# Second layer in place and by chunks, last attention block by token groups, maxima over partitions on TensorE, and one normalization moved to GpSimd

## Chip, cores and metric

One core of a Trainium2 chip runs the whole program. The metric is device time in microseconds (us). Before the change three runs took 737.27, 738.0 and 739.08 us, median 738.0. Five engines work side by side, each through its own queue in program order: TensorE (PE) multiplies matrices, VectorE (DVE) and ScalarE (ACT) do elementwise work and reductions, GpSimd (POOL) does elementwise work, and SyncE (SP) only issues transfers. ACT can issue transfers too. An engine passes its work on to another through semaphores, and an instruction that waits at the head of a queue holds all that stand behind it.

## What is computed

A gated block: cross-attention of 4096 tokens of width 512 over a context of 77 rows, then a feed-forward net of width 2048 whose two linear layers round their input and their weights to integers, with one scale for a whole tensor. Cut to what matters:

```python
def _quant_per_tensor(x):
    scale = jnp.maximum(jnp.max(jnp.abs(x)), 1e-6) / 127.0
    return round(x / scale), scale

def _qlinear(x2d, w, b):
    xq, sx = _quant_per_tensor(x2d)
    wq, sw = _quant_per_tensor(w)
    return (xq @ wq.T + b) * (sw * sx)

x = x + tanh(g_xattn) * attention(layernorm(x), ctx, ctx)   # 16 heads of 32
n = layernorm(x)
h = gelu(_qlinear(n, w1, b1))
x = x + tanh(g_ffn) * _qlinear(h, w2, b2)
```

Each maximum runs over a whole tensor. So the first layer can't begin before the last token has left the attention, and the second can't begin before the last hidden value is known.

## The kernel before

The tokens are cut into NB = 8 blocks of 512, each held on chip as four groups of 128 tokens: `X[i]`, [128, 4, 512] f32. Everything happens in one program, in three stages.

**Attention.** A loop over the blocks, inside it eight steps `s`. The order on PE and DVE is partly written out by hand (`tc.issue_after`); a scheduling layer places the rest. In each step `softmax` (L248) gets scores from PE, subtracts the maximum on DVE, takes the exponential on ACT and the sum on DVE, and has GpSimd multiply by the reciprocal (L275); PE transposes the result (`transpose_a`), multiplies by the values (`apply_v`), and projects (`project_o`, L307) into `po`; DVE adds that to X (L317). `norm2` (L321) makes the statistics of the new X (`mean2`, `rstd2`; GpSimd takes the power -1/2 at L140) and the largest normalized value of the block, `xmax`. In blocks 1 to 4 the weights of the feed-forward net are loaded, their maxima are taken (`weight_max`, L350), and they are rounded to `w1q` and `w2q`. `scale_of` (L142) turns maxima of 128 partitions into one scale: DVE reduces within a partition, GpSimd reduces over the partitions with `partition_all_reduce` (L148), and DVE makes the scale and its inverse. For the last block there is no next block to work beside: four projections, then one `norm2` for all four groups (L468 to L470).

**First layer.** `quantize_x` (L496) normalizes a block again into `xs`, rounds it into `xq` (adding and subtracting a large constant), transposes it on PE into `px`, and DVE copies it to `xqT`. For each block, 16 hidden chunks of 128 follow: four matmuls into half of a `ph` tile (two tiles of two halves), the gelu on ACT with scale `s1` (L536), and for each pair of chunks a maximum on DVE (`hmax`, L543). Four chunks make a tile `G` of 1 MB. The tiles of blocks 0 to 5 go out to DRAM (L554, issued by SP); the eight of blocks 6 and 7 are held in the eight buffers of `gpool` (HELD = 8).

**Second layer.** Blocks in the order 6, 7, 0, ... 5 (L566). Each tile, held or loaded back into a free `gpool` buffer as `Gb` (L573, issued by SP), is scaled in place on ACT (L574) and rounded on DVE into `hq` (L575; two buffers). For each token group GpSimd adds the bias to X (L579), 16 matmuls accumulate in `po`, which the profile calls `pf` (two PSUM buffers), DVE makes `o = pf * s2 + X` (L590; two buffers of `opool`), and ACT's queue issues the store of `o` (L592).

Of the kernel before, what the change touches and what calls it, by code (L numbers as in the profile page):

```python
# [8 lines left out]
F32 = mybir.dt.float32  # L9
# [6 lines left out]
P = 128  # L16
# [23 lines left out]
def tile_flamingo_gated_block(  # L40
# [78 lines left out]
    identb = const.tile([P, P], BF16, name="identb")  # L119
    nc.vector.tensor_copy(identb, ident)  # L120
    mhalf = const.tile([P, NT], F32, name="mhalf")
    nc.gpsimd.memset(mhalf, -0.5)
# [4 lines left out]
    rstd2 = const.tile([P, NB, NT], F32, name="rstd2")  # L127
    xmax = const.tile([P, NB], F32, name="xmax")
    hmax = const.tile([P, NB, GT, 2], F32, name="hmax")

    def layernorm_stats(xb, mv, rstd, name):

        n = xb.shape[1]
        st = small.tile([P, n, 6], F32, tag="st", name=f"st_{name}")
        for t in range(n):
            nc.vector.bn_stats(st[:, t, :], xb[:, t, :])
            nc.vector.bn_aggr(mv[:, t, :], st[:, t, :])
        ve = small.tile([P, n], F32, tag="ve", name=f"ve_{name}")
        nc.vector.tensor_scalar(ve, mv[:, :, 1], EPS, None, ALU.add)
        nc.gpsimd.tensor_tensor(rstd, ve, mhalf[:, :n], ALU.pow)  # L140

    def scale_of(maxima, name):  # L142


        m = const.tile([P, 1], F32, name=f"m_{name}")
        nc.vector.tensor_reduce(m, maxima, AX.X, ALU.max)
        g = const.tile([P, 1], F32, name=f"g_{name}")
        nc.gpsimd.partition_all_reduce(g, m, P, bass_isa.ReduceOp.max)  # L148
        s = const.tile([P, 1], F32, name=f"s_{name}")
        nc.vector.tensor_scalar(s, g, MIN_RANGE, 1.0 / QP, ALU.max, ALU.mult)  # L150
        inv = const.tile([P, 1], F32, name=f"inv_{name}")
        nc.vector.reciprocal(inv, s)
        return s, inv

    def quantize(dst, src, inv):

        nc.vector.tensor_scalar(src, src, inv, MAGIC, ALU.mult, ALU.add)
        nc.vector.tensor_scalar(dst, src, MAGIC, None, ALU.subtract)

# [4 lines left out]
    with actx:  # L164
# [155 lines left out]

        def norm2(i):  # L321
            xb = X[i]
            layernorm_stats(xb, mean2[:, i, :, :], rstd2[:, i, :], f"f{i}")
            tm = small.tile([P, NT], F32, tag="tm", name=f"tm{i}")
            for t in range(NT):
                xn = work.tile([P, D], F32, tag="xn", name=f"xf{i}_{t}")
                nc.vector.tensor_scalar(
                    xn,
                    xb[:, t, :],
                    mean2[:, i, t, 0:1],  # L330
                    rstd2[:, i, t : t + 1],
                    ALU.subtract,
                    ALU.mult,
                )
                nc.vector.tensor_reduce(
                    tm[:, t : t + 1], xn, AX.X, ALU.max, apply_absolute_value=True
                )
            nc.vector.tensor_reduce(xmax[:, i : i + 1], tm, AX.X, ALU.max)

# [10 lines left out]
        def weight_max(name, j):  # L350
            if j == 0:
                wmax[name] = const.tile([P, 4], F32, name=f"max_{name}")
            nc.vector.tensor_reduce(
                wmax[name][:, j : j + 1],
                wraw[name, j],
                AX.XY,
                ALU.max,
                apply_absolute_value=True,
            )
            if j == 3:  # L360
                s_w[name], inv_w[name] = scale_of(wmax[name], name)

# [6 lines left out]
        def weight_step(i, s):  # L369
            j, odd = divmod(s, 2)  # L370
            if i == 1 and odd:
                weight_max("w1", j)
            if i == 2 and odd:
                quantize(w1q[:, :, j * TB : (j + 1) * TB], wraw["w1", j], inv_w["w1"])
# [31 lines left out]
        for i in range(NB):  # L406
            for s in range(2 * NG):
                last = None
                if s + 1 < 2 * NG:
                    last = softmax(i, s + 1)  # L410
                elif i + 1 < NB:
                    last = softmax(i + 1, 0)
# [39 lines left out]
                if s == 7 and i > 0:  # L452
                    norm2(i - 1)
                if last is not None:
# [10 lines left out]
            if i == 2:  # L465
                load_w("w2", w2_piece, range(2))
        apply_v(NB - 1, NG - 1)
        for t in range(NT):  # L468
            project_o(NB - 1, t)
        norm2(NB - 1)  # L470
    s_w1, s_w2 = s_w["w1"], s_w["w2"]


    s_x, inv_x = scale_of(xmax, "x")
    s1 = const.tile([P, 1], F32, name="s1")
    nc.vector.tensor_tensor(s1, s_x, s_w1, ALU.mult)
    b1s = const.tile([P, FC], F32, name="b1s")
    nc.vector.tensor_scalar(b1s, b1_sb, s1, None, ALU.mult)

    gpool = ctx.enter_context(tc.tile_pool(name="gpool", bufs=HELD))  # L480
    hidden_dram = ctx.enter_context(
# [7 lines left out]

    held, stored = {}, {}  # L490
    with ExitStack() as fctx:
        fwork = fctx.enter_context(tc.tile_pool(name="fwork", bufs=2))
        ps_h = fctx.enter_context(tc.tile_pool(name="ps_h", bufs=2, space=PSUM))
        ps_x = fctx.enter_context(tc.tile_pool(name="ps_x", bufs=2, space=PSUM))

        def quantize_x(i):  # L496
            xs = fwork.tile([P, NT, D], F32, tag="xs", name=f"xs{i}")
            xq = fwork.tile([P, NT, D], BF16, tag="xq", name=f"xq{i}")
            xqT = fwork.tile([P, KC, TB], BF16, tag="xqT", name=f"xqT{i}")
            for t in range(NT):  # L500
                nc.vector.tensor_scalar(
                    xs[:, t, :],
                    X[i][:, t, :],
                    mean2[:, i, t, 0:1],
                    rstd2[:, i, t : t + 1],
                    ALU.subtract,
                    ALU.mult,
                )
            quantize(xq, xs, inv_x)
            for t in range(NT):  # L510
                px = ps_x.tile([P, KC, P], BF16, tag="px", name=f"px{i}_{t}")
                for kc in range(KC):
                    nc.tensor.transpose(px[:, kc, :], xq[:, t, kc * P : (kc + 1) * P], identb)
                nc.vector.tensor_copy(xqT[:, :, t * P : (t + 1) * P], px)
            return xqT

        xqT = quantize_x(0)
        for i in range(NB):
            cur = xqT
            if i + 1 < NB:  # L520
                xqT = quantize_x(i + 1)
            for a in range(GT):
                G = gtile(f"G{i}_{a}")
                for v in range(GF // 2):
                    ph = ps_h.tile([P, 2, TB], F32, tag="ph", name=f"ph{i}_{a}_{v}")
                    for u in range(2):
# [15 lines left out]
                        )  # L542
                    nc.vector.tensor_reduce(  # L543
                        hmax[:, i, a, v : v + 1],
                        G[:, 2 * v : 2 * v + 2, :],
                        AX.XY,
                        ALU.max,
                        apply_absolute_value=True,
                    )
                if i * GT + a >= NB * GT - HELD:  # L550
                    held[i, a] = G
                else:
                    stored[i, a] = hidden_dram.tile([P, GF, TB], F32, name=f"h{i}_{a}")
                    nc.sync.dma_start(stored[i, a], G)  # L554
    s_h, inv_h = scale_of(hmax.rearrange("p b a v -> p (b a v)"), "h")
    s2 = const.tile([P, 1], F32, name="s2")
# [3 lines left out]


    hpool = ctx.enter_context(tc.tile_pool(name="hpool", bufs=2))
    opool = ctx.enter_context(tc.tile_pool(name="opool", bufs=2))
    ps_o = ctx.enter_context(tc.tile_pool(name="ps_o", bufs=2, space=PSUM))
    first = NB - HELD // GT
    for i in [*range(first, NB), *range(first)]:  # L566
        hq = hpool.tile([P, FC, TB], BF16, tag="hq", name=f"hq{i}")
        for a in range(GT):
            if (i, a) in held:
                G = held[i, a]  # L570
            else:
                G = gtile(f"Gb{i}_{a}")
                nc.sync.dma_start(G, stored[i, a])  # L573
            nc.scalar.activation(G, G, AF.Copy, bias=MAGIC, scale=inv_h)  # L574
            nc.vector.tensor_scalar(  # L575
                hq[:, a * GF : (a + 1) * GF, :], G, MAGIC, None, ALU.subtract
            )
        for t in range(NT):
            nc.gpsimd.tensor_tensor(X[i][:, t, :], X[i][:, t, :], b2_sb, ALU.add)  # L579
            po = ps_o.tile([P, D], F32, tag="po", name=f"pf{i}_{t}")  # L580
            for fc in range(FC):
                nc.tensor.matmul(  # L582
                    po,
                    hq[:, fc, t * P : (t + 1) * P],
                    w2q[:, fc, :],
                    start=(fc == 0),
                    stop=(fc == FC - 1),
                )
            o = opool.tile([P, D], F32, tag="o", name=f"o{i}_{t}")
            nc.vector.scalar_tensor_tensor(o, po, s2, X[i][:, t, :], ALU.mult, ALU.add)  # L590
            r = i * TB + t * P
            nc.scalar.dma_start(out[r : r + P, :], o)  # L592

# [61 lines left out]
```

## Time and profile before

| What | From the profile |
|---|---|
| profiled execution | 735.06 us, of which the span from first to last instruction is 733.3 us |
| mean granted PE clock over the span | 0.977 |
| busy: PE, DVE, ACT, POOL | 670.1, 516.0, 342.4, 198.8 us |
| attention, to the end of the last `po` | to 448.4 us |
| first layer, from the first matmul into `ph` to PE's last | 467.4 to 594.4 us |
| second layer, from the first matmul into `pf` to PE's last | 601.3 to 729.3 us |
| loads `Gb`, 24 of 1 MB | 4.7 / 7.5 / 10.9 us from issue to landing (min / median / max) |
| stores of `out`, 32 of 256 KB | 2.0 / 2.7 / 10.4 us |

A profile page names a group of instructions by its line in the code, engine, operation and tiles (`out<-in`, buffer numbers left out). A timeline row has its start, its length, and in brackets how long the engine sat idle before it and what released it. A row of waits reads: who waited, for whom, us in total, number of times, longest. The clock row gives the share of full speed that PE was granted. PE's ends are modelled, and some matmul records are missing, so counts of matmuls in a row can be a little low.

### The profile page before, as it was taken

To read this page: it belongs to the slowest core of one execution; us is meant where nothing else is said; L and a number is where in the kernel's file an instruction comes from. 1 tells how busy PE (TensorE), PEld (TensorE's weight loads), DVE (VectorE), ACT (ScalarE), POOL (GpSimd) and SP (SyncE) were. 2 spreads that over 40 slices of the span, in tenths; PEclk is the share of its full clock that TensorE was granted. 3 is DMA by queue.
4 is the path that set the end of the run, shared out by engine and by line. 5 is a ranking of instruction groups with operands and counts; after the bars stand their busy time and mean duration, and the time that the engine had idled before them with its cause. 6 is when DMAs were issued, how large, how long until landed. Compare 5 with 4: busy or idle time off the path is not lost.

```text
span 733.3 us, 7847 instructions
## 1 busy us (share of the span) xinstructions
PE 670.1 (91%) x2873; PEld 332.7 (45%) x2896; DVE 516.0 (70%) x807; ACT 342.4 (47%) x467; POOL 198.8 (27%) x161
## 2 busy tenths in 40 slices
PE   4999999999999899999999994699999969889897
PEld 2655545454544454555555541344444424334343
DVE  3563688789798699677677576999986666665442
ACT  1444444334433433444344420377777877655500
POOL 3133332342331442333332320000000009980000
PEclk9999999999999999999999998799999979989999
DMA  9901100111320321100000000166666019888621
GB/s 287 341 0 57 59 1 1 58 58 58 114 87 29 115 78 43 52 0 1 0 1 2 0 1 0 53 258 263 278 260 265 1 50 404 348 296 327 253 86 72
DMA packets 26430, 85.40 MB, mean 116 GB/s; under 512 B 3531, under 2 KB 3531, under 8 KB 20248
## 3 DMA queue, kind: packets, MB, share of 16 engines
q1 hardware_dynamic: 19912, 75.15, 26.7%
q10 hardware_dynamic: 6480, 9.76, 3.7%
q8 instruction: 23, 0.38, 0.2%
q14 instruction: 15, 0.12, 0.0%
HBM read 51.34 MB, written 33.55 MB: 116 GB/s over the span
## 4 chain that ended last, share of the span: by engine, by line
PE 64%; DVE 19%; DMA 6%; POOL 5%; ACT 5%; issue 2%; SPq 0%; POOLq 0%; DVEq 0%; ACTq 0%
PE ph L529 16%; PE pq L238 10%; PE po L310 10%; PE pf L582 10%; PE pta L288 6%; PE ps L254 6%; DMA out_y<-o 5%; POOL e L275 3%; PE pc L297 3%; DVE mx L263 2%; DVE sm L272 2%; DVE e L267 2%; ACT G L574 1%; DVE hq L575 1%; DVE o L590 1%
## 5 line engine op out<-in xcount | busy, mean ns | idle before, releaser
L275 POOL TENSOR_TENSOR e<-e,rs 128x616 f32<-128x616 f32 x64 | 78.9, 1234 | 247.1 <-DVE rs L274 184.5
L582 PE MATMUL pf<-w2q,hq 128*128 128x512 bf16 x502 | 117.7, 393 | 17.2 <-DVE o L590 9.6
L529 PE MATMUL ph<-xqT,w1q 128*128 128x512 bf16 x499 | 121.2, 378 | 2.4 <-ACT G L536 1.6
L238 PE MATMUL pq<-xnT,wq_sb 128*128 128x512 f32 x256 | 119.8, 605 | 0.7 <-ACT xnT L230 0.7
L289 ACT COPY aT<-pta 77x512 f32<-77x512 f32 x128 | 73.1, 581 | 93.8 <-PE pta L288 93.6
L310 PE MATMUL po<-wo_sb,cT 128*128 128x512 f32 x256 | 116.4, 593 | 0.0
L536 ACT ACTIVATE G<-ph,b1s,s 128x512 f32<-128x512 f32 x128 | 99.5, 778 | 25.8 <-PE ph L529 20.6
L288 PEld LDWEIGHTS pta<-ident,e 128*77 128x77 f32 x512 | 59.9, 148 | 67.5 <-POOL e L275 33.0
L288 PE MATMUL pta<-ident,e 128*77 128x128 f32 x512 | 79.3, 281 | 12.1 <-POOL e L275 9.7
L543 DVE TENSOR_REDUCE hmax<-G 128x1 f32<-128x1024 f32 x64 | 75.1, 1214 | 20.1 <-ACT G L536 19.9
L582 PEld LDWEIGHTS <-hq 128*128 128x128 bf16 x512 | 51.1, 100 | 83.8 <-issue 19.1
L263 DVE TENSOR_REDUCE mx<-ps 128x8 f32<-128x616 f32 x64 | 50.4, 787 | 44.0 <-PE ps L254 44.0
L529 PEld LDWEIGHTS <-w1q 128*128 128x128 bf16 x512 | 49.0, 97 | 67.9 <-issue 17.6
L254 PE MATMUL ps<-kb,qT 128*128 128x308 f32 x256 | 78.8, 428 | 0.5 <-ACT kb L193 0.4
L270 ACT ACTIVATE e<-e 128x616 f32<-128x616 f32 x64 | 45.9, 716 | 55.8 <-DVE e L267 51.4
L272 DVE TENSOR_REDUCE sm<-e 128x8 f32<-128x616 f32 x64 | 50.5, 790 | 27.9 <-ACT e L270 27.7
L238 PEld LDWEIGHTS pq<-xnT,wq_sb 128*128 128x128 f32 x256 | 46.7, 193 | 50.7 <-issue 47.5
L310 PEld LDWEIGHTS po<-wo_sb,cT 128*128 128x128 f32 x256 | 46.5, 190 | 46.5 <-issue 45.1
L590 DVE SCALAR_TENSOR_TENSOR o<-pf,s,x 128x512 f32<-128x512 f32 x32 | 23.9, 747 | 59.9 <-DMA out_y<-o 37.4
L574 ACT ACTIVATE Gb<-Gb,inv_h 128x2048 f32<-128x2048 f32 x24 | 47.2, 1997 | 31.8 <-DVE o L590 31.6
L267 DVE TENSOR_TENSOR e<-ps,mx 128x616 f32<-128x616 f32 x64 | 50.9, 796 | 6.0 <-POOL e L275 3.4
L579 POOL TENSOR_TENSOR x<-x,b_sb 128x512 f32<-128x512 f32 x32 | 52.6, 1679 | 7.0 <-issue 7.0
(73 smaller groups left out, 612.9 us busy)
## 6 DMA issues: line engine op xcount, KB each, us to landing
h<-G SPq DMA_DIRECT2D x24, 1024.0 KB, 3.9
Gb<-h SPq DMA_DIRECT2D x24, 1024.0 KB, 7.5
raw_w<-in_w2T SPq DMA_DIRECT2D x8, 1024.0 KB, 5.0
out_y<-o ACTq DMA_DIRECT2D x32, 256.0 KB, 2.7
x<-in_x SPq DMA_DIRECT2D x7, 1024.0 KB, 5.0
raw_w<-in_w1T SPq DMA_DIRECT2D x4, 1024.0 KB, 9.7
x<-in_x SPq DMA_DIRECT2D x4, 256.0 KB, 5.8
wq_sb<-in_wqT ACTq DMA_DIRECT2D x1, 1024.0 KB, 11.2
```

Of the source, the lines that this page charges most:

```text
L238: nc.tensor.matmul(pq, wq_sb[:, kc, g * P : (g + 1) * P], xnT[i][:, kc, :], start=(kc == 0), stop=(kc == KC - 1),)
L254: nc.tensor.matmul(ps[:, u, :GK], qT[i, g][:, t * P : (t + 1) * P], kblk[i // NBB][:, g, :], start=True, stop=True,)
L267: last["DVE"] = nc.vector.tensor_tensor(e4, sc, mx[:, :, :, None].to_broadcast([P, 2, HG, NK]), ALU.subtract).ins
L272: nc.vector.tensor_reduce(sm, e4, AX.X, ALU.add)
L275: last["POOL"] = nc.gpsimd.tensor_tensor(e4, e4, rs[:, :, :, None].to_broadcast([P, 2, HG, NK]), ALU.mult).ins
L288: nc.tensor.transpose(pt[:NK, j, :], es[i, s][:, u, j, :], ident)
L289: nc.scalar.copy(aT[i, g][:, :, t * P : (t + 1) * P], pt[:NK, :, :])
L310: nc.tensor.matmul(po, cT[i, g][:, t * P : (t + 1) * P], wo_sb[:, g, :], start=(g == 0), stop=(g == NG - 1),)
L529: nc.tensor.matmul(ph[:, u, :], w1q[:, kc, fc * P : (fc + 1) * P], cur[:, kc, :], start=(kc == 0), stop=(kc == KC - 1),)
L536: nc.scalar.activation(G[:, 2 * v + u, :], ph[:, u, :], AF.Gelu, bias=b1s[:, fc : fc + 1], scale=s1,)
L543: nc.vector.tensor_reduce(hmax[:, i, a, v : v + 1], G[:, 2 * v : 2 * v + 2, :], AX.XY, ALU.max, apply_absolute_value=True,)
L582: nc.tensor.matmul(po, hq[:, fc, t * P : (t + 1) * P], w2q[:, fc, :], start=(fc == 0), stop=(fc == FC - 1),)
```

## The change

- `scale_of` no longer uses GpSimd. DVE multiplies the identity by the column of maxima, PE multiplies a matrix of ones by that diagonal, which puts all 128 maxima into each partition's row of a PSUM tile, and DVE takes the maximum of the row. For the weights the call moves to the first step of the next block.
- The last attention block is handled group by group: statistics after each projection, and the maximum of one group after the statistics of the next. The gelu's table is loaded on ACT by a one-column activation (`warm`) right after the last `cT`.
- Block 0's normalization for the first layer, `xs`, is put on GpSimd, with a raised priority and behind the last product of the softmax. Its rounding goes group by group, the last two groups partly on ACT, which also does the four copies to `xqT`. Other blocks keep DVE; their normalization stands behind the rounding of the block ahead.
- The very last pair's `hmax` is taken in two halves.
- The second layer adds into X and stores from X; `opool` is gone, `ps_o` has four buffers, and SP's queue issues the stores. In its first block the chunk is the outer loop and the four groups the inner one, and the first chunk is rounded by DVE alone.
- Several pools of the later stages get `reuse_waits="tile"`, and `gpool` is put on the other side of the memory.

The diff, cut to its core:

```diff
-    def scale_of(maxima, name):
+    def scale_of(maxima, name, psum, tag):
         m = const.tile([P, 1], F32, name=f"m_{name}")
         nc.vector.tensor_reduce(m, maxima, AX.X, ALU.max)
+        diag = small.tile([P, P], F32, tag="diag", name=f"diag_{name}", bufs=1)
+        nc.vector.tensor_scalar(diag, ident, m, None, ALU.mult)
+        pg = psum.tile([P, 512], F32, tag=tag, name=f"pg_{name}")
+        nc.tensor.matmul(pg[:, :P], ones, diag, start=True, stop=True)
         g = const.tile([P, 1], F32, name=f"g_{name}")
-        nc.gpsimd.partition_all_reduce(g, m, P, bass_isa.ReduceOp.max)
+        nc.vector.tensor_reduce(g, pg[:, :P], AX.X, ALU.max)
...
-            if j == 3:
-                s_w[name], inv_w[name] = scale_of(wmax[name], name)
...
+            if i in (2, 4) and s == 0:
+                name = "w1" if i == 2 else "w2"
+                s_w[name], inv_w[name] = scale_of(wmax[name], name, ps_p, "pp")
...
+        warm = small.tile([P, 1], F32, tag="warm", name="warm")
+        nc.scalar.activation(warm, cT[NB - 1, NG - 1][:, 0:1], AF.Gelu)
         for t in range(NT):
             project_o(NB - 1, t)
-        norm2(NB - 1)
+            last = norm2_stats(NB - 1, t, t + 1)
+            if t > 0:
+                with tc.issue_after(last):
+                    norm2_max(NB - 1, t - 1, t)
+        norm2_max(NB - 1, NT - 1, NT)
...
+        def quantize_x(i, xs, n):
+            xq = fwork.tile([P, NT, D], BF16, tag="xq", name=f"xq{i}")
+            xqT = fwork.tile([P, KC, TB], BF16, tag="xqT", name=f"xqT{i}")
+            for t0 in range(0, NT, n):
+                v, vq = xs[:, t0 : t0 + n, :], xq[:, t0 : t0 + n, :]
+                if n == 1 and t0 >= NT // 2:
+                    nc.scalar.activation(v, v, AF.Copy, bias=MAGIC, scale=inv_x)
+                    last = nc.vector.tensor_scalar(vq, v, MAGIC, None, ALU.subtract).ins
+                else:
+                    last = quantize(vq, v, inv_x)
+                for t in range(t0, t0 + n):
...
+                    if n == 1:
+                        nc.scalar.copy(dst, px)
+                    else:
+                        nc.vector.tensor_copy(dst, px)
+            return xqT, last
+        with tc.issue_after(last_product), tc.high_priority(offset=300):
+            xs = normalize_x(0, nc.gpsimd)
+        s_x, inv_x = scale_of(xmax, "x", ps_g, "pg")
+        xqT, last = quantize_x(0, xs, 1)
...
-    opool = ctx.enter_context(tc.tile_pool(name="opool", bufs=2))
-    ps_o = ctx.enter_context(tc.tile_pool(name="ps_o", bufs=2, space=PSUM))
+    ps_o = ctx.enter_context(tc.tile_pool(name="ps_o", bufs=NT, space=PSUM))
...
+            done = 0
+            if (i, a) == (first, 0):
+                quantize(hq[:, 0, :], G[:, 0, :], inv_h)
+                done = 1
+            rest = G[:, done:, :]
+            nc.scalar.activation(rest, rest, AF.Copy, bias=MAGIC, scale=inv_h)
             nc.vector.tensor_scalar(
-                hq[:, a * GF : (a + 1) * GF, :], G, MAGIC, None, ALU.subtract
+                hq[:, a * GF + done : (a + 1) * GF, :], rest, MAGIC, None, ALU.subtract
             )
...
+        if i == first:
+            for fc in range(FC):
+                for t in range(NT):
+                    accumulate(t, fc)
         for t in range(NT):
-            nc.gpsimd.tensor_tensor(X[i][:, t, :], X[i][:, t, :], b2_sb, ALU.add)
...
-            o = opool.tile([P, D], F32, tag="o", name=f"o{i}_{t}")
-            nc.vector.scalar_tensor_tensor(o, po, s2, X[i][:, t, :], ALU.mult, ALU.add)
+            y = X[i][:, t, :]
+            nc.gpsimd.tensor_tensor(y, y, b2_sb, ALU.add)
+            if i != first:
+                for fc in range(FC):
+                    accumulate(t, fc)
+            nc.vector.scalar_tensor_tensor(y, po[t], s2, y, ALU.mult, ALU.add)
             r = i * TB + t * P
-            nc.scalar.dma_start(out[r : r + P, :], o)
+            nc.sync.dma_start(out[r : r + P, :], y)
```

`normalize_x(i, engine)` (L517 of the changed kernel) is the loop of four normalizations that stood in `quantize_x`, L501 before and L520 after; `accumulate(t, fc)` is one matmul of L582, with `po[t]` allocated at its first chunk.

## The prediction

> **What bounds the kernel now.** I read the page first, then the waits, then the stretches in which TensorE (PE) is not fed. The page has PE at 91% of the span, so only what leaves PE idle, or running slowly, can be won. From the waits:
>
> ```profile
> DVE o L590 <- DMA out_y<-o: 37.4, 10, 7.4
> ACT Gb L574 <- DVE o L590: 31.6, 14, 6.1
> PE pf L582 <- DVE o L590: 9.6, 6, 2.9
> PE pf L582 <- DVE hq L575: 6.8, 1, 6.8
> ```
>
> The chain to see: a store of `out` (256 KB beside the 1 MB loads) holds one of two `o` buffers; VectorE (DVE) waits for it, and ScalarE (ACT), which issues the stores in order, and PE, which has two PSUM buffers, wait for DVE. PE's own timeline of the second layer, with the idle time before each piece in brackets:
>
> ```profile
> 601.25 24.27 PE L582 MATMUL pf<-w2q,hq 128*128 128x512 bf16 x94 [6.83 <-DVE hq L575]
> 626.16 3.61 PE L582 MATMUL pf<-w2q,hq 128*128 128x512 bf16 x16 [0.64 <-DVE o L590]
> 630.59 7.07 PE L582 MATMUL pf<-w2q,hq 128*128 128x512 bf16 x31 [0.82 <-DVE o L590]
> 639.34 3.61 PE L582 MATMUL pf<-w2q,hq 128*128 128x512 bf16 x16 [1.69 <-DVE o L590]
> 645.84 23.82 PE L582 MATMUL pf<-w2q,hq 128*128 128x512 bf16 x94 [2.88 <-DVE o L590]
> 670.34 14.22 PE L582 MATMUL pf<-w2q,hq 128*128 128x512 bf16 x63 [0.68 <-DVE o L590]
> 687.45 41.86 PE L582 MATMUL pf<-w2q,hq 128*128 128x512 bf16 x188 [2.89 <-DVE o L590]
> ```
>
> At the end, where nothing disturbs, DVE's L590 rows follow each other by 3.45 us (722.50, 725.95, 729.40), which is one group of 16 matmuls. 32 groups make 110.4 us; the stage took 729.3 - 601.25 = 128.05. The six waits are 9.6 of the missing 17.65. The table by stretches (columns: length; PE, weight load, DVE, ACT, GpSimd busy; granted clock; DMA share; GB/s) shows most of the rest:
>
> ```profile
> 597.00:601.00 4.00, 0.00 (x0) 0.00 (x0) 2.06 (x6) 3.07 (x2) 0.35 (x1) 0.53 0.00 0
> 605.00:608.00 3.00, 3.00 (x10) 1.19 (x9) 2.01 (x2) 3.00 (x3) 3.00 (x2) 0.59 0.97 352
> 612.00:616.00 4.00, 3.95 (x19) 1.82 (x19) 1.85 (x2) 3.23 (x2) 4.00 (x3) 1.00 1.01 390
> 646.00:648.00 2.00, 2.00 (x6) 0.66 (x5) 1.99 (x2) 1.74 (x1) 2.00 (x2) 0.50 1.11 328
> 684.00:688.00 4.00, 1.11 (x6) 0.45 (x5) 0.75 (x1) 0.13 (x1) 0.00 (x0) 1.00 1.00 416
> ```
>
> After two idle stretches PE gets half its clock for some 6 us each: about 6 us lost. The last 2 us are waits for `hq` in the first block.
>
> The second place is the seam between attention and first layer, where one thing runs at a time:
>
> ```profile
> 450.47 1.01 POOL L140 TENSOR_TENSOR rstd<-ve_f,mhalf 128x4 f32<-128x4 f32 x1 [17.08 <-DVE ve_f L139]
> 457.28 0.64 POOL L148 PARTITION_ALL_REDUCE g_x<-m_x  x1 [5.80 <-DVE m_x L146]
> 463.71 1.01 PE L513 MATMUL px<-identb,xq 128*128 128x128 bf16 x8 [15.26 <-DVE xq L158]
> 468.66 1.28 ACT L536 ACT_TABLE_LOAD   x1 [33.48 <-PE ph L529]
> 470.78 4.59 PE L529 MATMUL ph<-xqT,w1q 128*128 128x512 bf16 x19 [1.19 <-ACT G L536]
> ```
>
> PE ends its last `po` at 448.4; `m_x` ends at 456.5, `inv_x` at 459.38; the third pair of hidden chunks, from which the layer keeps its pace, starts at 470.78.
>
> **The change, part by part.**
>
> *Second layer.* Results go into X, so the `o` buffers and their 37.4 us of waits are gone; four PSUM buffers instead of two cover DVE's 0.75 us per group. What is late next? (a) PE itself. (b) The loads: 24 MB in, 8 MB out. They now share SP's queue with the stores, in a fixed order: five loads, four stores of block 6, then about one load per store. A store waits for its group, and the load behind it waits too. By PE's pace of 3.45 us per group, `Gb2`'s last piece is issued near 640 and wanted near 659 (15 us after 4 us for ACT and DVE are taken off), `Gb5`'s last near 688.5 and wanted near 700.4, 8 us after the same. Landing took 4.7/7.5/10.9 us (min/median/max), and at 688 little else moves, so this fits. The rate fits too: 1 MB and 256 KB per 3.45 us is 380 GB/s, against 415 to 426 in the busiest stretches, and the first five loads are early. (c) ACT: 2.0 us per tile, 32 tiles, half of the stage. GpSimd's 32 additions are the same.
>
> The start: PE's first layer ends at E (594.40 before). The last gelu ends at E+0.83, a half-size maximum (half of 1.21) at E+1.5, `m_h` (0.22) E+1.75, the diagonal (128 columns, about 0.2) E+2.0, one f32 product E+2.5, a maximum over 128 (0.25) E+2.8, `s_h` and `inv_h` (0.15 each) E+3.2: before, E+3.43. Then DVE quantizes one chunk of 512 twice (0.45 each, as L501's 2.36 for 5) with two `s2` steps between: PE starts at E+4.5, before at E+6.85. Block 6 then runs chunk by chunk into four banks: 13.8 us, plus 2.3 for half clock over 4.6 us, plus 0.4 for the bank that DVE frees: E+20.9. 28 groups of 3.45 make E+117.5; before E+134.9. **Gain 17.4 us.** The tail (0.75, then 3.1 us for the last store) is the same.
>
> Here the skill is weighed. "TensorE: Matmul & The Clock Gate", Part 1, says that half clock follows an idle window of about 3.4 us that runs free. E to E+4.5 is split by the product at E+2.4 into two shorter pieces, so by the rule PE might stay warm, and the gain be 19.7. The rows: 2.88 us of idle time before 645.84 cost the clock, 2.89 before 687.45 did not. I take the cold start.
>
> *Seam.* Each token group's statistics and maximum now follow its projection; with `po` ending at 438.1, 441.6, 445.0 and 448.4, only group 3 is left at 448.5, and its `ve_f` ends at 450.4. By that alone `m_x` would end near 453.5, 3 us early. But in the built order GpSimd (POOL) has: third `rstd`, the **four normalizations** of block 0, fourth `rstd`. Nothing else holds them, so they start at 447.8 and the fourth `rstd` waits behind all four; DVE's last `xf`, two maxima and all that follows wait for it. Their price is not in the trace. The nearest row is one operation with one column:
>
> ```profile
> L429 POOL TENSOR_SCALAR bo_sb<-bo_sb,tg 128x512 f32<-128x512 f32 x1 | 1.6, 1581 | 0.0
> ```
>
> The new one has two of each: from 1.58 to twice that, 3.2. I take 1.9, near the row. Then `rstd` ends at 447.85 + 7.6 + 0.7 = 456.2, `xf`, two `tm` (1.3), two `xmax`, `m_x`: 458.5. "GPSIMD Engine Reference", section 4.1, speaks against the change twice: elementwise work belongs on VectorE, and a reduction over partitions on GpSimd; but it calls one-input operations "roughly line-rate", an estimate of 0.5 us each like DVE's 0.47, with which `m_x` would end near 453.5. The row of 1.58 decides. For the reduction: by the row, `m_h` to `s_h` took 0.48 us by GpSimd; the three steps above take about 1.05. It is dearer by 0.6, and I have counted it.
>
> From `m_x`: diagonal, product at half clock, maximum, `s_x`, `inv_x`: 1.8, so 460.3 (before 459.38). Then, DVE and ACT sharing: `xq` of the first group at +1.5, last at +2.85; transposes; four ACT copies of 0.6, ending at +4.7; first product +4.8, two pairs, one partly at half clock, third pair at +9.3 = 469.6. The table load (1.28) is done in ACT's idle 33 us. Before: 470.78. **Gain 1.2 us**; 2.4 at 1.58 us each, a loss of 4.0 at 3.2. The first layer's pace, 1.89 us per pair, is not touched.
>
> *Weight maxima.* After the all-reduces POOL's next product starts 6.8 and 8.0 us later (132.80 to 139.59, 238.57 to 246.54), and PE idles 1.70 and 1.84 us. That goes. In exchange DVE holds in its queue for the product, which stands behind the transposes of `e`, and then `rs`, which POOL waits for, about 0.6 us late, and `mx` 2 us late. The two blocks took 53.08 and 53.24 us, the one between, without a reduction, 52.69, so there is little to win: I take 0, ends a gain of 3.5 and a loss of 3.
>
> **Sum:** 17.4 + 1.2 + 0 = 18.6. The profiled execution took 735.06 (span 733.3), so 716.5 on its scale. The runs' median, 738.0, lies 2.9 above it; on that scale 719.4, rounded to **719.5**.
>
> **Rivals.**
> 1. *GpSimd's normalizations cost 3.2 us each.* For it: two operations; DVE's fast forms hold POOL up (L579 1.68 beside them, the same shape 1.33 at L233). Against: nothing shows a second operation costing as much as the first. 724.7.
> 2. *The transfers become the bound.* For it: DMA share 1.0 from 603 to 632 and 397 GB/s at 660 to 670; and SP issues no load between about 608 and 616, while four stores wait. 33.5 MB at the 336 GB/s of 660 to 690 take 100 us: loads end near 700, block 5 follows: 9 us given back, 728.
> 3. *Slower: stores and loads lock each other in SP's queue.* If every load lands late, PE waits in each of six blocks. It decides when landing passes 15 us, and costs more than it brings when it passes 18 in all six blocks (3.1 us each). Largest seen: 10.9. 740.
> 4. *Better:* PE stays warm and the weight stalls are won: 714.
> 5. *It doesn't do what it says:* the buffers weren't the bound. Against: ten waits named. 738.
>
> **Chances.** Forecast 0.63 (own range 716 to 723), rivals 0.15, 0.12, 0.04, 0.05, 0.01. Range 714 to 728. About 0.3% (2 us) is what a measurement can tell from no change: faster 0.95, within 0.01, slower 0.04.
>
> **What would show it.** Right: no wait for `out_y` on DVE; PE from `inv_h` to the end in one piece of about 113 us at clock 1.0 after the first block; the fourth `rstd` starting only after four POOL rows at L520, about 6 to 9 us after the third. Wrong: PE `pf` waiting for `hq` or DMA in blocks 2 to 5 (rival 2 or 3); POOL rows over 2.5 us (rival 1); the two blocks with weight maxima over 54 us.

## The result and the profile after

| | median, us | runs | ratio to before (95% interval) |
|---|---|---|---|
| before, beside the first | 737.63 (737.23 to 739.08) | 4 | |
| changed | 726.75 (from 726.12) | 4 | 0.9846 (0.9827 to 0.9865) |
| before, beside the repeat | 736.54 (735.57 to 740.14) | 11 | |
| changed, repeated | 727.98 (725.44 to 730.48) | 4 | 0.9876 (0.9848 to 0.9903) |

Faster by 10.9 and 8.6 us, where 18.5 were forecast. One of the first four runs was disturbed (791.95 us at a lower clock; the median of the other three is 726.58), and it was the profiled one, so the profile below is that of the repeat (span 723.5 us).

From here on E is the moment at which PE ends the first layer, in each profile its own, and the seam is the stretch between attention and first layer. Cut by stage, the two profiles stand like this:

| stage | before | predicted | changed |
|---|---|---|---|
| last `po` to first `ph` | 18.99 | | 16.48 |
| first `ph` to E | 126.97 | | 128.55 |
| E | 594.41 | 593.2 | 594.16 |
| E to first `pf` | 6.84 | 4.5 | 4.94 |
| E to PE's end | 134.90 | 117.5 | 125.03 |

So nearly all that was won lies behind E (9.9 us of 17.4 predicted). Of the 2.5 us that the seam won, 1.6 were given back in the first layer and 0.7 in the attention (its last `po` ends at 449.13, before at 448.45). In the waits of the changed kernel no row for `out_y` or `o` is left on DVE. In their place (columns: who, for whom, us in total, times, longest):

```profile
ACT Gb L627 <- DMA Gb<-h: 43.5, 18, 7.6
...
DVE hq L628 <- ACT Gb L627: 31.8, 16, 4.3
```

PE's timeline of the second layer, idle time before each piece in brackets:

```profile
599.10 1.87 PE L636 MATMUL pf<-w2q,hq 128*128 128x512 bf16 x4 [1.96 <-DVE hq L165]
601.47 14.21 PE L636 MATMUL pf<-w2q,hq 128*128 128x512 bf16 x59 [0.50 <-DVE hq L628]
617.67 71.82 PE L636 MATMUL pf<-w2q,hq 128*128 128x512 bf16 x325 [1.99 <-DVE x L654]
690.56 13.12 PE L636 MATMUL pf<-w2q,hq 128*128 128x512 bf16 x59 [1.07 <-DVE hq L628]
703.97 1.04 PE L636 MATMUL pf<-w2q,hq 128*128 128x512 bf16 x4 [0.29 <-DVE hq L628]
707.79 11.40 PE L636 MATMUL pf<-w2q,hq 128*128 128x512 bf16 x51 [2.78 <-DVE hq L628]
```

The six waits for `o` of before are gone, and PE keeps its pace for 71.8 us. Then, in the last two blocks, it waits for `hq`, that is for loads. There is also 1.99 us between block 6 and block 7, which the prediction had at 0.4.

Why the loads are late shows in SP's own timeline (a row of several issues starts with the first):

```profile
620.05 0.40 SPq L621 DMA_DIRECT2D Gb<-h  x1
624.55 4.76 SPq L656 DMA_DIRECT2D out_y<-x  x2
629.41 0.38 SPq L621 DMA_DIRECT2D Gb<-h  x1
...
691.19 0.99 SPq L656 DMA_DIRECT2D out_y<-x  x2
692.27 0.44 SPq L621 DMA_DIRECT2D Gb<-h  x1
696.14 0.33 SPq L656 DMA_DIRECT2D out_y<-x  x1
696.56 0.40 SPq L621 DMA_DIRECT2D Gb<-h  x1
```

Almost every load goes out right behind a store, and the store goes out when DVE has made its sum. Between 620.5 and 629.4 no load is issued. The last one leaves at 696.56; the prediction had it at 688.5. On DVE the sums stand in turn behind roundings, which wait for loads. These are the rounding and the sum ahead of the store at 696.14:

```profile
694.22 1.23 DVE L628 TENSOR_SCALAR hq<-Gb 128x2048 bf16<-128x2048 f32 x1 [2.41 <-ACT Gb L627]
695.37 0.74 DVE L654 SCALAR_TENSOR_TENSOR x<-pf,s,x 128x512 f32<-128x512 f32 x1
```

The sum did not wait for PE, it stood behind the rounding, and that one behind ACT, which waited for a load. That is a ring: load, rounding, sum, store, next load.

The seam, on GpSimd and DVE:

```profile
448.46 8.24 POOL L520 TENSOR_SCALAR xs<-x,mean,rstd 128x512 f32<-128x512 f32 x4
456.68 0.55 POOL L142 TENSOR_TENSOR rstd<-ve_f,mhalf 128x1 f32<-128x1 f32 x1
```
```profile
457.26 0.55 DVE L338 TENSOR_SCALAR xf<-x,mean,rstd 128x512 f32<-128x512 f32 x1 [5.70 <-POOL rstd L142]
```

As predicted, four normalizations stand ahead of the fourth `rstd` (2.07 us each, 1.9 predicted), and DVE sits idle 5.70 us for it.

### The profile page after: what moved, and what is told of

Read it like the earlier page. It is cut to its first block, busy times and chain, and to the rows that moved or that the text cites. A ratio compares the mean times of both kernels' runs of the same rounds, so it can differ in the third digit from the quotient of the medians.

```text
span 790.0 us, 7864 instructions
## 1 busy us (share of the span) xinstructions
PE 750.2 (95%) x2881; PEld 358.1 (45%) x2904; DVE 530.3 (67%) x821; ACT 347.3 (44%) x474; POOL 210.0 (27%) x164
## 4 chain that ended last, share of the span: by engine, by line
PE 89%; DVE 4%; ACT 2%; POOL 2%; DMA 1%; issue 1%; SPq 0%; POOLq 0%; ACTq 0%; DVEq 0%
PE pf L636 16%; PE ph L574 16%; PE pq L245 16%; PE po L317 15%; PE ps L261 9%; PE pta L295 9%; PE pc L304 4%; PE ptx L236 1%; PE px L544 1%; POOL xs L520 1%; PE pvv L208 1%; DMA x<-in_x 1%; DVE mx L270 1%; POOL e L282 1%; PE pk L188 1%
## 5 line engine op out<-in xcount | busy, mean ns | idle before, releaser
L245 PE MATMUL pq<-xnT,wq_sb 128*128 128x512 f32 x256 | 137.3, 682 | 0.7 <-ACT xnT L237 0.7
L317 PE MATMUL po<-wo_sb,cT 128*128 128x512 f32 x256 | 135.1, 673 | 0.0
L574 PE MATMUL ph<-xqT,w1q 128*128 128x512 bf16 x499 | 132.3, 419 | 1.9 <-ACT xqT L547 0.7
L636 PE MATMUL pf<-w2q,hq 128*128 128x512 bf16 x502 | 129.9, 426 | 3.4 <-DVE hq L165 2.0
L295 PEld LDWEIGHTS pta<-ident,e 128*77 128x77 f32 x512 | 67.3, 154 | 64.9 <-issue 35.4
L591 DVE TENSOR_REDUCE hmax<-G 128x1 f32<-128x1024 f32 (+1 forms) x65 | 75.4, 1198 | 23.5 <-ACT G L581 23.1
L295 PE MATMUL pta<-ident,e 128*77 128x128 f32 x512 | 86.5, 299 | 3.7 <-POOL e L282 2.4
L261 PE MATMUL ps<-kb,qT 128*128 128x308 f32 x256 | 89.4, 474 | 0.4 <-ACT kb L200 0.4
L253 ACT ACTIVATE qT<-pq,bq_sb 128x512 f32<-128x512 f32 x32 | 22.0, 687 | 82.5 <-PE pq L245 82.5
L654 DVE SCALAR_TENSOR_TENSOR x<-pf,s,x 128x512 f32<-128x512 f32 x32 | 23.7, 748 | 50.8 <-PE pf L636 47.5
```

The source lines that it names most:

```text
L245: nc.tensor.matmul(pq, wq_sb[:, kc, g * P : (g + 1) * P], xnT[i][:, kc, :], start=(kc == 0), stop=(kc == KC - 1),)
L261: nc.tensor.matmul(ps[:, u, :GK], qT[i, g][:, t * P : (t + 1) * P], kblk[i // NBB][:, g, :], start=True, stop=True,)
L295: nc.tensor.transpose(pt[:NK, j, :], es[i, s][:, u, j, :], ident)
L317: nc.tensor.matmul(po, cT[i, g][:, t * P : (t + 1) * P], wo_sb[:, g, :], start=(g == 0), stop=(g == NG - 1),)
L574: nc.tensor.matmul(ph[:, u, :], w1q[:, kc, fc * P : (fc + 1) * P], cur[:, kc, :], start=(kc == 0), stop=(kc == KC - 1),)
L591: nc.vector.tensor_reduce(hmax[:, k + u : k + u + 1], G[:, 2 * v + u : 2 * v + u + n, :], AX.XY, ALU.max, apply_absolute_value=True,)
```

## Experiments

All are compared with the kernel before on the same chip. a0 to e3 ran on one chip, e4 to e7 on a second and e8 to e11 on a third. The stage columns are from one profile each. "Seam" runs from the last `po` to the first `ph`, "layer 1" from there to E. "Warm" says that PE's granted clock is kept at 1.00 ahead of the layer, "cold" that the layer starts at 0.50.

| run | median, us | ratio (95% interval) | seam | layer 1 | E to PE's end |
|---|---|---|---|---|---|
| a0, changed again | 727.98 | 0.9876 (0.9848 to 0.9903) | 16.48 | 128.55 | 125.03 |
| e1, `xs` earlier | 724.03 | 0.9829 (0.9804 to 0.9855) | 11.16 | 128.08 | 125.54 |
| e2, weights by GpSimd | 725.74 | 0.9840 (0.9815 to 0.9865) | 16.52 | 128.57 | 125.70 |
| e3, stores by ACT | 721.41 | 0.9788 (0.9765 to 0.9811) | 16.49 | 128.57 | 120.30 |
| e4, e3 with `o` again | 732.92 | 0.9948 (0.9930 to 0.9966) | 16.49 | 128.52 | 131.18 |
| e5, loads first on SP | 720.14 | 0.9769 (0.9754 to 0.9784) | 16.48 | 127.87 | 120.27 |
| e6, e3, one sum ahead | 719.54 | 0.9763 (0.9745 to 0.9780) | 16.48 | 127.51 | 119.60 |
| e7, e3, additions held | 719.77 | 0.9766 (0.9751 to 0.9781) | 16.48 | 127.58 | 117.95 |
| e8, e3, `xs` on DVE | 715.75 | 0.9723 (0.9706 to 0.9740) | 12.46 | 127.94 | 120.31 |
| e9, e8 and e7 | 715.33 | 0.9716 (0.9698 to 0.9734) | 12.46 | 127.61 | 119.65 |
| e10, e9, warm layer 2 | 712.69 | 0.9682 (0.9664 to 0.9700) | 12.45 | 127.95 | 117.48 |
| e11, e10, warm layer 1 | **711.10** | **0.9660 (0.9640 to 0.9680)** | 11.73 | 126.33 | 117.47 |

The end of the attention itself moved between 448.5 and 452.5 us from profile to profile, so single spans are not compared, only stages and medians.

### Four first experiments

**a0.** No edit.

> The changed kernel once more, for a profile at the full clock. Theory S (the second layer gives less than the 17.4 us that were summed, because transfers and not TensorE set its pace): TensorE ends the second layer 122 us or more after its end of the first, with waits for hq, and time 726 to 727. Theory W (the weight maxima cost the missing 7 us in blocks 2 and 4): the second layer takes 117 to 118, and blocks 2 and 4 take 56 us or more each, where they took 53.1 and 53.2.

PE ends 125.03 us after E, with waits for `hq`, and blocks 2 and 4 take 53.82 and 53.49 us, not 56: theory S holds, W doesn't. The median is 1 us above the band of S.

**e1.** Block 0's `xs` goes into the dead `wq_sb` and stands on GpSimd behind block 6's `rstd`, ahead of all four of the last block. The other blocks share one `xs` buffer instead of two.

```diff
...
+            if i == 0:
+                xs = wq_sb
...
-        with tc.issue_after(last_product), tc.high_priority(offset=300):
+        with tc.issue_after(powers[f"f{NB - 2}_0"]), tc.high_priority(offset=300):
```

> Block 0's normalization is written into the dead wq_sb, so that GpSimd can do it behind block 6's rstd and ahead of all four rstd of block 7. If the four normalizations of 2.07 us each, standing ahead of the last rstd, are what holds m_x, this is 4 to 5 us faster than the changed kernel (721.5 to 722.5). If something else at the seam sets the start of the first layer (DVE, the rounding, the transposes), it is the same within 1 us.

The seam became 5.3 us shorter, and DVE waits 0.44 us for the last `rstd`. The median is 4.0 below a0's, though 1.5 above the expected band, and the two intervals just touch; the seam carries this reading. In the profile the attention ended 3.4 us later than in a0 (see the last section), which took most of the gain back there.

**e2.** The scales of the two weights by GpSimd's all-reduce again, at their old place.

```diff
+            if j == 3:
+                s_w[name], inv_w[name] = scale_of_gpsimd(wmax[name], name)
...
-            if i in (2, 4) and s == 0:
...
```

> The changed kernel with the weights' two scales taken by GpSimd at the old place. Theory W: 6 to 7 us faster than the changed kernel (719 to 721). Theory S: the same within 1 us, or up to 3.5 us slower if the stalls of 1.7 and 1.84 us after the all-reduces come back in full.

The intervals of e2 and a0 overlap: no difference that the medians can tell. The two blocks took 53.07 and 53.16 us here, against 53.82 and 53.49 in a0. So by the profiles the new way costs 0.75 and 0.33 us there, 1.1 together, inside the bounds put on it.

**e3.** The stores are issued by ACT, as before the change.

```diff
-            nc.sync.dma_start(out[r : r + P, :], y)
+            nc.scalar.dma_start(out[r : r + P, :], y)
```

> The changed kernel with the 32 stores issued by ScalarE instead of SyncE. If loads that stand behind waiting stores in SyncE's queue hold the second layer (one form of theory S), this is 4 to 7 us faster. If TensorE sets its pace (theory W), it is the same within 1 us, or slower, since ScalarE then waits for VectorE's sums again.

SP's timeline and PE's, of e3:

```profile
601.72 67.84 SPq L621 DMA_DIRECT2D Gb<-h  x24
```
```profile
601.72 14.26 PE L636 MATMUL pf<-w2q,hq 128*128 128x512 bf16 x59 [0.51 <-DVE hq L628]
617.90 96.85 PE L636 MATMUL pf<-w2q,hq 128*128 128x512 bf16 x439 [1.93 <-DVE x L654]
```

All 24 loads are out by 669.6, and from 617.90 PE runs in one piece of 96.85 us; 28 groups at 3.45 are 96.6. E to the end is 4.7 us shorter, and the median 6.6 below a0's, inside what was expected. The 1.93 us after block 6 stay.

### What the second layer's gain consists of, and what it lacks

**e4.** e3 with the two `o` buffers back; four banks and the chunk-by-group first block stay.

```diff
+    opool = ctx.enter_context(tc.tile_pool(name="opool", bufs=2))
...
-            nc.vector.scalar_tensor_tensor(y, po[t], s2, y, ALU.mult, ALU.add)
+            o = opool.tile([P, D], F32, tag="o", name=f"o{i}_{t}")
+            nc.vector.scalar_tensor_tensor(o, po[t], s2, y, ALU.mult, ALU.add)
...
-            nc.scalar.dma_start(out[r : r + P, :], y)
+            nc.scalar.dma_start(out[r : r + P, :], o)
```

> As e3 (stores issued by ScalarE), but the results go into two o buffers again as before the change; four PSUM banks and the chunk-by-group first block stay. Theory (the two o buffers were the bound of the old second layer): VectorE waits for out_y again, some 10 times; with four banks TensorE covers more of each wait than with two, so 5 to 9 us come back: 726.5 to 730. Rival (the two extra PSUM banks alone were what helped): 721 to 723, and TensorE still runs in one piece.

Its waits:

```profile
DVE o L656 <- DMA out_y<-o: 40.5, 14, 6.9
ACT Gb L628 <- DVE o L656: 35.1, 10, 7.8
```

Adding into X is worth 10.9 us of the stage (131.18 against 120.30), more than expected: four banks don't cover waits of up to 6.9 us. Banks, first block and start bring the other 3.7 (134.90 to 131.18). The time missed the expected band by 2.9 us on the slow side; the waits are of the kind expected, 14 of them rather than 10.

**e5.** The changed kernel, all stores on SP's queue, but the stores of a block stand behind loads of a later one.

```diff
+        if len(late) == 2 * NT or i == first - 1:
+            with tc.issue_after(load):
+                for dst, y in late[:NT]:
+                    nc.sync.dma_start(dst, y)
+            late = late[NT:]
...
-            nc.sync.dma_start(out[r : r + P, :], y)
+            late.append((out[r : r + P, :], y))
...
```

> The changed kernel with all stores still on SyncE's queue, but the four stores of a block stand behind the loads for the block two later, so that no load ever stands behind a store that waits for its sum. Theory (it is the order within SP's queue that held the loads): as e3, 720.5 to 723; loads all issued by about 672. Rival (a second queue issues or moves more): stays at 726 to 728.

SP's timeline of e5:

```profile
659.32 3.27 SPq L622 DMA_DIRECT2D Gb<-h  x4
662.97 10.08 SPq L635 DMA_DIRECT2D out_y<-x  x4
673.14 3.90 SPq L622 DMA_DIRECT2D Gb<-h  x4
```

E to the end is 120.27, e3's 120.30. One queue carries it all as well as two, if its order lets four loads out between four stores. Loads still stand behind stores here, for up to 10 us, and the last leaves at 677 rather than 672; but then four go at once, early enough. So it was the order, not the queue or the transfers.

**e6 and e7** ask what the 1.9 us after block 6 are. In e6 DVE's order changes: the first sum of block 6 ahead of the eighth rounding, the other three behind it. In e7 that order stays, and GpSimd's additions for later blocks are held back.

```diff
...
+            with tc.issue_after(only) if behind else nullcontext():
+                rounded = nc.vector.tensor_scalar(
...
+                with tc.issue_after(rounded):
+                    for t in later:
+                        finish(first, t, last_po[t])
...
```
```diff
...
+        if i == first + 1:
+            b2_late = hpool.tile([P, D], F32, tag="b2", name="b2_late", bufs=1)
+            with tc.issue_after(scaled):
+                nc.scalar.copy(b2_late, b2_sb)
...
-            nc.gpsimd.tensor_tensor(y, y, b2_sb, ALU.add)
+            nc.gpsimd.tensor_tensor(y, y, b2_sb if i == first else b2_late, ALU.add)
```

> As e3, but VectorE's order is changed at one place: the first sum of block 6 stands ahead of the eighth rounding, the other three behind it. Theory (TensorE's 1.9 us idle after block 6 is VectorE's order): the idle goes to about 0.2, 719.5 to 720. Rival (the eighth rounding is then too late for the last four chunks of block 7): the idle moves into block 7, 721 to 721.5.

> As e3, with VectorE's order as it was, but GpSimd's additions for all blocks after the first wait until ScalarE has scaled the eight held tiles (they read a copy of b2 made behind the eighth scaling). Theory (GpSimd's additions beside VectorE stretch the eight roundings from 1.23 to 2.1 us): the first four or five roundings stay near 2.1, the later ones come at ScalarE's pace of 1.9 and end near 614.4 instead of 617.2; the idle after block 6 goes: 719.5 to 720. Rival (roundings are long for another reason): 721 to 722.

PE's row behind block 6 and DVE's row of the first sum, first of e6, then of e7; last, the first sums of e3:

```profile
618.36 96.85 PE L651 MATMUL pf<-w2q,hq 128*128 128x512 bf16 x448 [0.27 <-DVE x L617]
617.55 0.75 DVE L617 SCALAR_TENSOR_TENSOR x<-pf,s,x 128x512 f32<-128x512 f32 x1 [1.45 <-PE pf L651]
```
```profile
616.67 96.85 PE L640 MATMUL pf<-w2q,hq 128*128 128x512 bf16 x448 [0.26 <-DVE x L658]
615.87 2.72 DVE L658 SCALAR_TENSOR_TENSOR x<-pf,s,x 128x512 f32<-128x512 f32 x4 [0.48 <-PE pf L640]
```
```profile
617.11 2.71 DVE L654 SCALAR_TENSOR_TENSOR x<-pf,s,x 128x512 f32<-128x512 f32 x4
```

The gap went to 0.27 us in e6 and 0.26 in e7. A short gap alone proves little: in e5 it was 0.74 with DVE's order unchanged, since PE ran block 6 longer at half clock there and came late. But in e3 and e5 the first sum starts 17.8 us after PE's first `pf`, right behind the last rounding, and in e6 and e7 it starts 17.1 and 15.4 us after it, with DVE waiting for PE. So both edits reach the gap. At equal clock it is worth 1.7 us: the stage fell by 0.7 in e6, where block 6's second piece took 1.0 us longer than in e3 (15.24 against 14.26), and by 2.4 in e7, where it took 0.7 less (13.59).

DVE's roundings of the held tiles, by groups (busy us in total, mean ns of one), first of e3, then of e7:

```profile
L628 DVE TENSOR_SCALAR hq<-G 128x2048 bf16<-128x2048 f32 x7 | 15.5, 2279 | 0.0
```
```profile
L628 DVE TENSOR_SCALAR hq<-G 128x2048 bf16<-128x2048 f32 x7 | 11.3, 1666 | 1.3 <-ACT G L627 1.2
```

In e7 the last four roundings took 1.21 to 1.23 us each, and two of them waited for ACT. The four that ran beside the additions stayed long (up to 2.31). GpSimd's additions beside the roundings are what makes them long, and the long roundings are what the sum stood behind. The kernel before shows the same, on GpSimd and on DVE:

```profile
604.46 37.37 POOL L579 TENSOR_TENSOR x<-x,b_sb 128x512 f32<-128x512 f32 x22 [7.01 <-issue]
```
```profile
603.75 1.23 DVE L575 TENSOR_SCALAR hq<-G 128x2048 bf16<-128x2048 f32 x1 [0.67 <-ACT G L574]
605.64 1.55 DVE L575 TENSOR_SCALAR hq<-G 128x2048 bf16<-128x2048 f32 x1 [0.66 <-ACT G L574]
607.54 1.88 DVE L575 TENSOR_SCALAR hq<-G 128x2048 bf16<-128x2048 f32 x1 [0.34 <-ACT G L574]
```

There GpSimd came to its additions only at 604.46, 7.01 us after its all-reduce, and until then a rounding took 1.23 us. In the changed kernel GpSimd has no reduction and starts adding at 599.3, beside the first rounding. The medians, 719.5 and 719.8, are those expected, but the intervals of e3, e6 and e7 overlap: it is these rows that carry the reading, not the medians.

### The seam, and the clock

**e8.** e3 with block 0's `xs` on DVE, where it fills the wait for the last `rstd`.

```diff
-        with tc.issue_after(last_product), tc.high_priority(offset=300):
-            xs = normalize_x(0, nc.gpsimd)
+        with tc.issue_after(last), tc.high_priority(offset=300):
+            xs = normalize_x(0, nc.vector)
```

> As e3, with the early normalization taken back from GpSimd: VectorE makes block 0's four xs rows while it waits for the fourth rstd. Theory (GpSimd's four rows hold the fourth rstd): from ve_f of group 3 at 451.0, four rows (1.9), two xf (1.0), two tm (1.3), two xmax and m_x (0.4): m_x ends at 455.5 instead of 459.4 on the scale of the changed kernel's profile, so 3.9 us earlier, 717 to 718. Rival (the rows only move from one engine's path to the other's): 720.5 to 722.

DVE's timeline of e8:

```profile
450.86 1.90 DVE L520 TENSOR_SCALAR xs<-x,mean,rstd 128x512 f32<-128x512 f32 x4
452.69 0.99 DVE L338 TENSOR_SCALAR xf<-x,mean,rstd 128x512 f32<-128x512 f32 x2
...
455.09 0.16 DVE L149 TENSOR_REDUCE m_x<-xmax 128x1 f32<-128x11 f32 x1
```

`m_x` stands 4.3 us after the last `ve_f`, in a0 8.3. The seam is 4.0 us shorter (12.46), the median 5.7, 1.3 below the expected band; by the ratios, which leave the chip out, it is 0.0065 of 737, or 4.8.

**e9 to e11** put things together. e9 is e8 with e7's hold. e10 adds e6's order and products of no use on PE, whose result is never read; e11 has 26 and 8 more of them, behind the last `po` and behind `pg_x`.

```diff
...
+    def fill(behind, n):
+        with tc.issue_after(behind):
+            for _ in range(n):
+                nc.tensor.matmul(pw, w2q[:, 0, :P], w2q[:, 0, :], start=True, stop=True)
...
+    fill(products["ph"], 9)
     s_h, inv_h = scale_of(hmax, "h", ps_g, "pg")
+    fill(products["pg"], 8)
```

> e8 with e7's held-back additions. If the two gains are of different places they add: 715.5 to 716.5. If not: as e8.

> e9, with e6's order (one sum ahead of the eighth rounding) and 9 + 8 products of no use on TensorE in the two idle stretches of 2.4 and 2.0 us between the layers (their result is never read). Theory (the half clock at the start of the second layer comes from these stretches): granted clock 1.0 from the first product into pf, block 6's 60 products in about 13.0 us, 2 us off: 713.5 to 714.5. Rival 1 (ScalarE's and VectorE's chain of scaling and rounding is what block 6 waits for, next behind the clock): TensorE waits for hq instead, no more than 0.5 us off. Rival 2 (the products of no use delay pg_h or the first product): no gain or a loss up to 1 us.

> e10, with 26 such products behind the last po and 8 behind pg_x. Theory (the new seam starts the first layer cold: 12 products took 4.6 us at half clock instead of 2.6): clock 1.0 there, 2 us off, 711.5 to 712.5. Rival (the transposes and their copies on ScalarE set the start of the layer, not the clock): less than 0.7 off e10.

The start of the second layer in two stretches of 2 us each (length; PE, weight load, DVE, ACT, GpSimd busy; granted clock; DMA share; GB/s), first a0, then e10:

```profile
601.10:603.10 2.00, 1.63 (x4) 0.57 (x5) 1.95 (x2) 2.00 (x2) 2.00 (x2) 0.50 0.35 61
603.10:605.10 2.00, 2.00 (x9) 0.88 (x8) 2.00 (x2) 2.00 (x2) 2.00 (x2) 0.85 0.87 365
```
```profile
596.30:598.30 2.00, 1.45 (x7) 0.70 (x8) 1.95 (x2) 2.00 (x2) 2.00 (x2) 1.00 0.26 33
598.30:600.30 2.00, 1.95 (x10) 0.88 (x9) 2.00 (x2) 2.00 (x2) 2.00 (x2) 1.00 0.83 340
```

PE's timeline where the second layer of e10 starts, then where the first layer starts, in e10 and in e11:

```profile
589.45 2.10 PE L610 MATMUL pw<-w2q 128*128 128x512 bf16 x9
592.04 0.49 PE L155 MATMUL pg_h<-diag_h,ones 128*128 128x128 f32 x2 [0.49 <-DVE diag_h L153]
592.37 1.89 PE L610 MATMUL pw<-w2q 128*128 128x512 bf16 x8
...
596.85 13.12 PE L666 MATMUL pf<-w2q,hq 128*128 128x512 bf16 x59 [1.49 <-DVE hq L650]
```
```profile
462.47 4.01 PE L576 MATMUL ph<-xqT,w1q 128*128 128x512 bf16 x11 [0.22 <-issue]
```
```profile
461.42 3.35 PE L585 MATMUL ph<-xqT,w1q 128*128 128x512 bf16 x13 [0.67 <-ACT xqT L556]
```

e10 keeps the clock at 1.00, block 6's last 59 products take 13.12 us (15.29 in e9), and the stage ends at E+117.48, 2.2 us earlier than in e9. The median falls by 2.6 us, 0.8 below the expected band. e6's order came in with the same run, but the gap after block 6 was already 0.27 in e9 and is 0.26 here, so the clock carries the gain. PE now waits 1.49 instead of 0.50 us for the second piece of `hq`: the next limit.

e11's first 13 products take 3.35 us, where the first 12 of e10 took 0.59 and 4.01, and the clock is 1.00 from 455 to 467, in e10 0.50 to 465. Layer 1 is 1.6 us shorter and the seam 0.7; the median fell by 1.6, with intervals that overlap. So the theory holds, by the stages with what was expected of it, by the median with less.

e9 can't be told from e8 by the medians: the additions bring 0.4 us there, not the 1.6 between e3 and e7. Its stage was 0.7 shorter than e8's. Block 6 ran long at half clock (15.29 us), so PE itself came late (the first sum waited 2.17 us for it) and hid what was won.

## Why the prediction was right, and where its sizes were off

- **Range and forecast.** The measured times lie inside the whole range, 714 to 728, but outside the forecast's own 716 to 723, to which 0.63 was given. That they come near rival 2's 728 is luck: its cause was not there (e3). Of the signs named, no wait for `out_y` and a fourth `rstd` 7.95 us after the third came true. PE in one piece did not, and PE waiting for `hq`, a sign of being wrong, came in blocks 4 and 5.
- **The bound and what goes with it: right.** Waiting for the two `o` buffers, which stores held, was the bound (e4: 10.9 us of the stage). DVE's waits for `out_y` are gone. One reading was off: 2 us were put down to waits for `hq` in the first block, but PE's first piece before, 24.27 us, shows no such idle time. The forecast doesn't use it.
- **"They fit" in SP's queue: the term that failed.** The step said that `Gb5`'s last load would be issued near 688.5 and have 8 us to spare. It left at 696.56. The step paced stores by PE alone; the ring through DVE's order adds to it. Price: 125.03 less 120.3, 4.7 us (e3, e5). The mechanism was rival 3's, stores and loads holding each other in SP's queue. What failed in rival 3 was its condition: landing took 4.7/7.8/11.3 us (min/median/max), not over 15, and the ring cost 4.7 us, not the whole gain. "Perfetto Trace Analysis", "DMA Optimizations", of the Trainium skill suggests one issuing engine for loads and another for stores; that spoke against this part of the change, and the prediction didn't weigh it. e3 agrees with it by 4.7 us. e5 shows that reordering does as much.
- **Block 6: 0.4 us for a bank was 2.0**, since the first sum stands behind eight roundings lengthened by GpSimd. Price: 0.7 us in e6 and 2.4 in e7, 1.7 in both at equal clock. Another 0.5 us is a wait for the second piece of `hq`, which the sum left out. The prediction held "GpSimd's 32 additions are the same"; they are, but without the all-reduce they start 5 us sooner and meet all eight roundings.
- **Start: E+4.94, not E+4.5.** In a0's DVE rows `m_h` ended at E+2.05 (1.75 predicted), since the last half-size maximum ended at E+1.80 and not 1.5: it stood behind a full one. `inv_h` ended at E+3.70 (3.2): diagonal and product took 0.1 us more each.
- **17.4 us of gain** would have needed E+117.5 (the terms as written add up to 117.6). e7 reached E+117.95, but on the shortest half clock of all; e9, with the same additions held, took 119.65. So the sum was right to about 0.5 to 2 us for a kernel without the ring and the additions, and 7.5 us too large for this one.
- **Cold start: right.** In a0 and e1 to e9, which have no products of no use, PE fell to 0.50, or stood at it, behind its start between E+4.72 and E+5.16, as was taken. It did not stay warm, though the rule of the Trainium skill's "TensorE: Matmul & The Clock Gate", Part 1, seemed to allow that (gain 19.7): here two idle stretches of 2.43 and 1.96 us with a product between them were enough (a0).
- **Seam: 1.2 predicted, 0.25 measured.** 1.9 us per normalization was 2.07, `m_x` ended at 459.4 rather than 458.5. The four of them cost 4.0 us of waiting against DVE (e8): the advice of "GPSIMD Engine Reference", 4.1, to keep elementwise work on VectorE was right by that much, while its "roughly line-rate" for operations with one input was not (2.07 us against 0.54 for the same row on DVE). Most of what was left went into the first layer, 128.55 against 126.97, which started cold: the prediction had counted one pair "partly at half clock"; 12 products were (e11 wins 1.6 us there). The attention's 0.7 us took the rest.
- **Weights' maxima at 0:** the medians can't tell it from 0 (e2). The profiles put it at a loss of 1.1 us, inside the ends given. In four profiles block 2 passed the 54 us that were named as a sign of being wrong (last section), for a total of some 2.5 us.
- **Rival 1** (3.2 us each): refuted by 2.07. **Rival 2** (the transfers are the bound): refuted by e3, which moves the same bytes with all loads issued by 669.6. **Rivals 4 and 5** didn't occur.

Counted to PE's end, 8.5 us are missing of 18.6: the ring 4.7, start and block 6 with the 28 groups behind it 2.8 (0.4, 2.1 and 0.3, by e3), and what stands ahead of E 1.0. The first median is 7.3 above the forecast, the second 8.5.

## What to carry to other kernels

When stores lose their own buffers, ask what now paces them: in a queue with a fixed order, a store that waits for compute holds every load behind it, so give loads another queue or let them go ahead in groups. An engine with time to spare isn't free if something short that others wait for stands behind the work given to it, or if it slows a neighbour: on GpSimd four normalizations cost 4.0 us of waiting, and additions that started earlier stretched DVE's roundings. Short idle stretches ahead of a dense stage on PE may be filled with products of no use, which here was worth 2.2 and 2.3 us by the stages (2.6 and 1.6 by the medians).

## What the runs showed of the hardware

- The half clock after the same start lasted differently from run to run. In 2 us stretches from the first `pf`, the clock rose again from 0.50 in the second stretch in e7, in the third in a0 to e4, and only in the fourth in e5, e6, e8 and e9. Block 6's second piece took 13.59 us in e7, 14.2 in a0 and e3, 15.4 and 15.2 in e5 and e6. So a single profile of this start is uncertain by some 2 us. The Trainium skill's "TensorE: Matmul & The Clock Gate", Part 1, says the activity window runs free of the program, so that the number of cold products varies between runs; these rows agree.
- An idle stretch of 2.0 us at the weights' maximum in block 2 (1.70 before) sometimes costs the clock. From 128 to 150 us e1, e6, e7 and e9 were granted 0.92 on average, those of the other experiments 1.00, and that block took 55.1 to 55.3 us instead of 53.8. Of e6, in stretches of 4 us:

```profile
132.00:136.00 4.00, 1.98 (x8) 0.81 (x7) 3.96 (x8) 1.40 (x2) 1.22 (x1) 1.00 0.01 2
136.00:140.00 4.00, 4.00 (x15) 3.05 (x13) 1.38 (x6) 1.16 (x2) 1.92 (x2) 0.57 0.00 0
```

The clock falls behind the idle stretch, not in it. Why it does so in four of the eleven profiles with the new way (e2 has the old one) and not in the rest stays open.
